# Filling the places behind the last edge on another engine, and issuing the products of types later, in a graph layer on one core

## The chip, the cores and the metric

The kernel runs on one core of a Trainium2 chip. The metric is the device time of one execution in microseconds (us). The kernel before takes 2105.05 us, the median of 3 runs (2102.25 to 2107.07).

A core has engines that run their own instruction streams in order and wait for one another by semaphores: TensorE (PE in the profile, its weight loads as PEld), VectorE (DVE), ScalarE (ACT), GpSimd (POOL) and SyncE (SP), which here issues plain transfers. Indirect transfers, that is gathers by a list of row numbers, are issued by GpSimd.

## The reference

There are 12500 nodes with 256 features each and 212500 edges, sorted by their target `dst`; each edge has a source and one of 8 types.

```python
h = jnp.maximum(_layernorm(x, axis=-1), 0.0)
hx = jnp.einsum('ni,rio->rno', h, weight)          # 8 x 12500 x 256
msg = hx[edge_type, src]
agg = segment_sum(msg, dst, num_segments=12500)
out = x + agg * 0.5**0.5 + h_bias + (h @ loop_weight) * 0.5**0.5
```

The last 12500 edges before the sort were loops from each node to itself; the sort is stable, so the loop of a node is the last of its edges. A loop has a type like any other edge.

## The kernel before

**Tiles of edges.** The kernel first writes h to memory (`norm_rows`), and then takes the edges in 1603 tiles of at most 128. Two tiles make a unit. For tile t, GpSimd gathers the 128 source rows of h (`gather`, L683), VectorE builds a one-hot of target and type for four tiles at once (`onehots`, L696), TensorE multiplies rows by one-hot into a PSUM bank of the unit (`edge_sums`, L723: two products, which the profile shows as four records), and VectorE adds the bank to a ring `acc` of sums by node and type in on-chip memory (`add_sums`, L735). There are four such banks.

The gather of tile t+58 (`AHEAD`) is written in the program in front of the work of tile t. There are buffers for 62 tiles (`MSGS`). The one-hots are made 8 tiles or more ahead (`LEAD`).

**Groups of nodes.** When all the edges of 128 nodes are in the ring, the group's output is made: 18 products with the weights and the loop weight (`product`, L883), handed out by a queue with due tiles among the tiles that follow. `finish` runs three tiles (`REST`) after the last of them. It adds the products to x (L894, L895), issues the store, and opens the slot of group g+6 in the ring: `begin` turns the rows of h of that group on TensorE into the bank `pt` (L759), copies them to `self_t` on ScalarE (L762), and in eight instructions on VectorE (L773) writes the loop's message, by its type, as the first summand. So loops are not gathered. There are 98 groups.

**Types of the loops.** `begin` has to know the type of each node's loop. For four groups at a time, `mark` prepares 0/1 patterns on VectorE; `find_types` multiplies them by a list of kinds (L800, into bank `pt`), finds the kind of each node in six small VectorE operations (L805 to L815), and writes four diagonal matrices on ScalarE (L818); `spread_types` turns these by one product (L825) and a copy (L827) into a row of types for all lanes. The bank `pt` has one buffer, which the turned rows, the products of types and the transposes of the preparation share. `find_types` is called in `finish` of every fourth group, after `begin`; `spread_types` is put into a list `late` with a due tile three tiles on. Entries of `late` are run in order once their tile is reached.

**Rounds of preparation.** Lists of rows, columns and places are made in 7 rounds of 128 units. Round b is prepared from 184 tiles (`PREP`) in front of its first tile: `load_indices` loads pieces of `src`, `dst` and `edge_type_8` into `nat_s`, `nat_d`, `nat_t`; `rises` (L366) subtracts neighbouring targets, and further VectorE steps follow, three steps every two tiles. The first three steps (the loads, `rises`, `stays`) stand in the same tile. In the last round not all of the 128 rows have edges: 33 rows are full, one has 41 edges and the others none. There the three arrays are filled first, and then loaded over. The fill of `nat_d` has to rise along the row, so that there are no edges with equal targets in it.

The work order on each engine is the order in which the program issues it.

Of the kernel before, what the change touches and what calls it, by code (L numbers as in the profile page):

```python
# [13 lines left out]
ALU = mybir.AluOpType  # L14
# [14 lines left out]
EDGES = 267  # L29
# [23 lines left out]
REST = 3  # L53
# [156 lines left out]
def kernel(  # L210
# [11 lines left out]
    nc = tc.nc  # L222
    N, D = x.shape
# [10 lines left out]
    EU = plan.EU  # L234
# [21 lines left out]
    line = const.tile([P, XG * GROUP], F32, name="line")  # L256
# [13 lines left out]
    with ExitStack() as main:  # L270
# [33 lines left out]
        def load_indices(b):  # L304

            rows_ = min(P, NU - b * P)
            last = b == NB - 1
            full = rows_ - last
            size = EDGES if b else U
            e0 = P * U + (b - 1) * P * EDGES if b else 0  # L310
            nat = {}
            for name, a, more in (("s", src, 0), ("d", dst, 1 if b else 0), ("t", etype, 0)):
                n = ep.tile([P, EDGES + 1], I32, name=f"nat_{name}")
                if last:

                    if more:
                        nc.gpsimd.iota(
                            n, pattern=[[2, EDGES + 1]], base=N - 2 * EU, channel_multiplier=0)
                    else:
                        nc.vector.memset(n, -1 if name == "d" else 0)  # L320
                if full:
                    nc.sync.dma_start(n[:full, : size + more], bass.AP(
                        tensor=a.tensor, offset=a.offset + e0, ap=[[size, full], [1, size + more]]))
                if last:
                    nc.sync.dma_start(
                        n[full : full + 1, :EU], a[E - EU : E].rearrange("(p q) -> p q", p=1))
                nat[name] = n
            return nat
# [416 lines left out]
        def clear(g):  # L745

            s0 = g % SLOTS * GROUP
            a = acc[:, :, :, s0 : s0 + GROUP].rearrange("p c r d -> p (c r) d")
            i = nc.scalar.activation(a, zero.unsqueeze(2).to_broadcast([P, KC * R, GROUP]), AF.Copy)
            zeroed[g, "slot"] = i.ins  # L750
# [14 lines left out]
        def begin(g):  # L765

            n = plan.ends[g] - plan.starts[g]
            q, k = divmod(g, XG)
            pst, copy = turn_nodes(g, selves)
            of = typed[q][:, k * GROUP : k * GROUP + n].unsqueeze(1).to_broadcast([P, KC, n])  # L770
            s0 = g % SLOTS * GROUP
            for r in range(R):
                i = nc.vector.scalar_tensor_tensor(  # L773
                    acc[:, :, r, s0 : s0 + n], of, float(r + 1), pst[:, :, :n],
                    op0=ALU.is_equal, op1=ALU.mult)
                if r == 0:
                    tc.add_manual_dep(i.ins, copy.name, SYNC_DEP, reason="one reader at a time")
            zeroed[g, "slot"] = i.ins
# [14 lines left out]
        def find_types(q):  # L793

            pt = ps_d.tile([P, 512], F32, tag="pt", name="ptt")
            pt = pt[:, : XG * (LASTS + 2)].rearrange("p (g k) -> p g k", g=XG)
            parts = [(b, m, i) for b, m in marked.pop(q) for i in range(2)]
            for g in range(XG):
                for b, m, i in parts:
                    nc.tensor.matmul(  # L800
                        pt[:, g, :], m[:, i, g * GROUP : (g + 1) * GROUP], loops[b][:, i, :],
                        start=(b, m, i) == parts[0], stop=(b, m, i) == parts[-1])

            place_ = small.tile([P, XG], F32, name="place_")
            nc.vector.tensor_scalar(  # L805
                place_, pt[:, :, LASTS], float(-plan.starts[XG * q]), None, op0=ALU.add)
            nc.vector.tensor_tensor(place_, place_, pt[:, :, LASTS + 1], op=ALU.add)
            nc.vector.tensor_tensor(place_, node, place_, op=ALU.subtract)
            one = small.tile([P, XG, LASTS], F32, name="one")
            nc.vector.tensor_tensor(  # L810
                one, line[:, :LASTS].unsqueeze(1).to_broadcast([P, XG, LASTS]),
                place_.unsqueeze(2).to_broadcast([P, XG, LASTS]), op=ALU.is_equal)
            nc.vector.tensor_tensor(one, one, pt[:, :, :LASTS], op=ALU.mult)
            kinds = small.tile([P, XG], F32, name="kinds")
            nc.vector.tensor_reduce(kinds, one, AX.X, ALU.add)  # L815
            marked[q] = marks.tile([P, XG * GROUP], BF16, name="diagonal")
            for g in range(XG):
                nc.scalar.activation(  # L818
                    marked[q][:, g * GROUP : (g + 1) * GROUP], ident, AF.Copy,
                    scale=kinds[:, g : g + 1])  # L820

        def spread_types(q):

            pt = ps_d.tile([P, 512], F32, tag="pt", name="ptt")
            nc.tensor.matmul(pt, ones_b, marked.pop(q), start=True, stop=True)  # L825
            typed[q] = types.tile([P, XG * GROUP], BF16, name="types")
            nc.scalar.activation(typed[q], pt, AF.Copy)  # L827
# [42 lines left out]
        def group_work(g):  # L870

            d0, n = plan.starts[g], plan.ends[g] - plan.starts[g]
            s0 = g % SLOTS * GROUP
            first_dep = [True]

            def product(r, c):
                if (r, c) == (R, 0):
                    got["out", g] = outs[g % 2][:, 0, :]
                if r == R:
                    lhs, rhs = got["self", g][:, c, :n], wl[:, c, :]  # L880
                else:
                    lhs, rhs = acc[:, c, r, s0 : s0 + n], w[:, c, r * D : (r + 1) * D]
                i = nc.tensor.matmul(got["out", g][:n], lhs, rhs, start=(r == R and c == 0),  # L883
                                     stop=(r == R - 1 and c == KC - 1))
                if (r, c) == (R, 0) and g < 2:
                    tc.add_manual_dep(i.ins, done["bias"], SYNC_DEP, reason="one engine at a time")
                if r < R and first_dep[0]:
                    first_dep[0] = False
                    tc.add_manual_dep(i.ins, added[plan.last[g]].name, SYNC_DEP, reason="sums complete")

            def finish():
                q, k = divmod(g, XG)
                rows_ = got["x", q]
                nc.vector.tensor_add(rows_[:n, k, :], rows_[:n, k, :], outs[g % 2][:n, 1, :])  # L894
                nc.vector.tensor_add(rows_[:n, k, :], rows_[:n, k, :], got["out", g][:n])  # L895
                if XG * (q + 1) >= plan.NG:
                    nc.sync.dma_start(out[d0 : d0 + n], rows_[:n, k, :])
                elif k == XG - 1:
                    first = plan.starts[XG * q]
                    nc.sync.dma_start(  # L900
                        out[first : d0 + n].rearrange("(k p) d -> p k d", p=P), rows_)
                b = g + SLOTS
                q, k = divmod(b, XG)
                if b < plan.NG:
                    if q < plan.typed:
                        clear(b)
                    else:
                        begin(b)
                if q + 1 >= plan.typed and XG * (q + 1) < plan.NG:
                    if k == XG // 4:  # L910
                        load_groups("h", h32, q + 1)
                    if k == XG - 2:
                        mark(q + 1)
                    if k == XG - 1:
                        find_types(q + 1)
                        done["late"].append((done["tile"] + REST, lambda: spread_types(q + 1)))

            def last():
                done["late"].append((done["tile"] + REST, finish))

            work = []
            for r in [R, *range(R)]:
                for c in range(KC):
                    work.append((0.55, lambda r=r, c=c: product(r, c)))
            work.append((0.0, last))
            return work

        with tc.manual_schedule():
# [46 lines left out]
            done = {"norm": 0, "weights": False, "late": [], "tile": 0}  # L975
# [39 lines left out]
            late = done["late"]  # L1015
# [113 lines left out]
```

## Time and profile before

| | |
|---|---|
| median of 3 runs | 2105.05 us |
| profiled execution, its own time | 2107.2 us |
| its span | 2105.2 us |
| TensorE busy | 1789.1 us, 85% |
| VectorE busy | 1327.7 us, 63% |
| GpSimd busy | 1523.2 us, 72% |
| ScalarE busy | 218.5 us, 10% |
| TensorE clock granted, mean | 0.92 of full speed |
| chain that ended last | TensorE 67%, VectorE 13%, issue 6%, transfers 6%, GpSimd 4% |

Times in the profile are counted from the start of the span. The slices are 40 equal parts of the span, 52.6 us each, with the busy share of an engine in tenths. A row of the waits has the waiting instruction, what released it, the total in us, the number of times and the longest. A row of the timeline has the start, the duration, the engine, the line, what is written and read, and in brackets the idle time of the engine before it and what ended it; a "q" behind an engine is its sequencer, where transfers are issued. A row of a table by stage has the stage, its length, for each engine the busy time and in brackets the number of records, then the granted TensorE clock, the transfers' share and their GB/s.

### The profile page before, as it was taken

The numbers are of one execution on the slowest core, as the hardware profiler recorded it, in microseconds if no ns is written. First come the engines' busy times: TensorE is split into PE (matmuls) and PEld (weight loads), VectorE is DVE, ScalarE is ACT, GpSimd is POOL, SyncE is SP. The second block draws the span as 40 slices with busy tenths as digits, with TensorE's granted clock in tenths as the row PEclk, the third lists the DMA queues.
The fourth block names the chain that finished last, engine by engine and source line by source line (L and its number), as shares of the span: only waits on it lengthen the run. The fifth ranks groups of instructions, "written<-read, shape, count | busy, mean of one in ns | idle before, by whom it ended". The sixth has DMA issues, their size and how long they took to land.

```text
span 2105.2 us, 29382 instructions
## 1 busy us (share of the span) xinstructions
PE 1789.1 (85%) x10411; PEld 1644.1 (78%) x10411; DVE 1327.7 (63%) x3274; ACT 218.5 (10%) x470; POOL 1523.2 (72%) x1630
## 2 busy tenths in 40 slices
PE   2468999998999998999988998988998860799998
PEld 2357998888898888888877887877888750698897
DVE  7869666668666687665686655577665520856652
ACT  7854100000000000000000000000000000000000
POOL 7767777777777777777777777777777777677750
PEclk8578999998999999999999999999999985899999
DMA  8963443443444344344344344343443433343430
GB/s 297 373 208 103 145 136 106 136 144 106 135 136 135 105 142 135 106 135 136 106 143 131 109 135 135 107 143 106 135 135 106 135 106 106 117 127 105 130 91 15
DMA packets 146904, 281.17 MB, mean 134 GB/s; under 512 B 28125, under 2 KB 95460, under 8 KB 146756
## 3 DMA queue, kind: packets, MB, share of 16 engines
q0 software_dynamic: 76944, 210.21, 34.2%
q1 hardware_dynamic: 69812, 69.05, 10.2%
q8 instruction: 85, 1.39, 0.3%
q14 instruction: 63, 0.52, 0.1%
HBM read 253.55 MB, written 25.60 MB: 133 GB/s over the span
## 4 chain that ended last, share of the span: by engine, by line
PE 67%; DVE 13%; issue 6%; DMA 6%; POOL 4%; ACT 2%; SPq 0%; DVEq 0%; ACTq 0%; POOLq 0%
PE ps L723 34%; PE po L883 31%; DMA msg<-h,gidx 4%; POOL msg L683 4%; DVE acc L773 3%; DVE acc L735 2%; DVE moves L349 2%; DVE fixed L350 2%; DMA h<-xt 1%; ACT xt L645 1%; DVE oh L696 1%; PE pst L759 1%; DMA w<-in_L_gnn_weight_dram 1%; DVE n_stats L633 0%; PE ptt L800 0%
## 5 line engine op out<-in xcount | busy, mean ns | idle before, releaser
L683 POOL DMA_INDIRECT msg<-h,gidx x1507 | 1430.0, 949 | 481.7 <-issue 396.3
L723 PE MATMUL ps<-oh,msg 128*128 128x176 f32 (+1 forms) x6412 | 1146.2, 310 | 187.5 <-DVE acc L735 76.6
L723 PEld LDWEIGHTS ps<-oh,msg 128*128 128x128 f32 x6412 | 1056.2, 198 | 290.1 <-issue 100.9
L883 PE MATMUL po<-w,acc 128*128 128x256 f32 x3136 | 892.7, 387 | 0.0
L696 DVE TENSOR_TENSOR oh<-fixed,cols 128x704 f32<-128x704 f32 x402 | 356.0, 886 | 356.2 <-PE ps L723 349.3
L883 PEld LDWEIGHTS po<-w,acc 128*128 128x128 f32 x3136 | 547.4, 195 | 25.3
L735 DVE TENSOR_TENSOR acc<-acc,ps 128x352 f32 x802 | 412.9, 515 | 180.9 <-PE ps L723 171.9
L773 DVE SCALAR_TENSOR_TENSOR acc<-types,pst 128x256 f32<-128x256 bf16 (+1 forms) x688 | 234.8, 414 | 74.5 <-ACT self_t L762 73.0
L762 ACT ACTIVATE self_t<-pst 128x256 f32<-128x256 f32 x98 | 37.5, 383 | 1524.5 <-PE pst L759 1524.5
L883 PE MATMUL po<-wl,self_t 128*128 128x256 f32 x392 | 121.2, 438 | 3.9 <-ACT self_t L762 2.4
L683 POOL DMA_INDIRECT msg<-in_x_dram,gidx x96 | 90.9, 947 | 31.1 <-issue 26.2
L883 PEld LDWEIGHTS po<-wl,self_t 128*128 128x128 f32 x392 | 75.7, 214 | 11.9 <-ACT self_t L762 2.8
L800 PE MATMUL ptt<-loops,mark 128*128 128x24 bf16 x216 | 9.3, 179 | 80.8 <-DVE acc L773 80.8
L800 PEld LDWEIGHTS <-mark 128*128 128x128 bf16 x216 | 7.3, 101 | 85.7 <-DVE acc L773 85.7
L366 DVE TENSOR_TENSOR rise<-nat_d 128x267 f32<-128x267 int32 x6 | 2.6, 432 | 79.0 <-DMA nat_d<-in_dst_dram 79.0
L645 ACT ACTIVATE xt<-xt,n_shift,n_rstd 128x256 f32<-128x256 f32 x98 | 50.9, 589 | 11.0 <-DVE n_shift L642 11.0
L645 ACT ACTIVATE msg<-msg,e_shift,e_rstd 128x256 f32<-128x256 f32 x96 | 49.6, 589 | 8.5 <-DVE e_shift L642 8.1
L894 DVE TENSOR_TENSOR xr<-xr,po 128x256 f32<-128x256 f32 x98 | 40.4, 412 | 7.4 <-PE po L883 7.4
L895 DVE TENSOR_TENSOR xr<-xr,po 128x256 f32<-128x256 f32 x98 | 41.2, 421 | 3.4
L818 ACT ACTIVATE diagonal<-ident,kinds 128x128 bf16<-128x128 f32 x88 | 28.1, 390 | 113.8 <-DVE kinds L815 113.8
L759 PE MATMUL pst<-ident,hr 128*128 128x128 f32 x196 | 37.7, 274 | 0.4 <-DVE offs L586 0.2
L349 DVE TENSOR_SCALAR moves<-fixed 128x267 int32<-128x267 int32 x84 | 36.4, 433 | 1.7
(200 smaller groups left out, 402.3 us busy)
## 6 DMA issues: line engine op xcount, KB each, us to landing
msg<-h,gidx POOLq DMA_INDIRECT x1507, 2.8
xt<-in_x_dram SPq DMA_DIRECT2D x24, 512.0 KB, 6.4
h<-xt SPq DMA_DIRECT2D x24, 512.0 KB
xr<-in_x_dram SPq DMA_DIRECT2D x24, 512.0 KB, 7.1
hr<-h SPq DMA_DIRECT2D x24, 512.0 KB, 6.3
out_dram<-xr SPq DMA_DIRECT2D x24, 512.0 KB, 4.0
w<-in_L_gnn_weight_dram SPq DMA_DIRECT2D x2, 1024.0 KB, 8.3
msg<-in_x_dram,gidx POOLq DMA_INDIRECT x96, 5.8
```

The lines of the kernel that those rows point to most:

```text
L349: nc.vector.tensor_single_scalar(m, packed, 1 << (bit + k), op=ALU.bitwise_and)
L350: nc.vector.copy_predicated(packed[:, : EDGES - (1 << k)], m[:, 1 << k :], packed[:, 1 << k :])
L645: nc.scalar.activation(rows_[j], rows_[j], AF.Relu, bias=shift[:n, j : j + 1], scale=rstd[:n, j : j + 1])
L683: nc.gpsimd.indirect_dma_start(out=msg[t], out_offset=None, in_=table[:, :], in_offset=bass.IndirectOffsetOnAxis(ap=gidx[b][:, at : at + 1 ...
L696: nc.vector.tensor_tensor(o[:, k : k + v, :i, :], iota_f.unsqueeze(1).unsqueeze(1).to_broadcast([P, v, i, C]), of.unsqueeze(3).to_broadcas ...
L723: nc.tensor.matmul(ps[:, c, from_ : from_ + width], m[:, c * P : (c + 1) * P], o[:, :width], start=(i == 0 and c == 0), stop=(end and c == ...
L735: i = nc.vector.tensor_tensor(a, a, ps, op=ALU.add)
L759: nc.tensor.transpose(pst[:, c, :n], rows_[:n, c * P : (c + 1) * P], ident[:n, :n])
L773: i = nc.vector.scalar_tensor_tensor(acc[:, :, r, s0 : s0 + n], of, float(r + 1), pst[:, :, :n], op0=ALU.is_equal, op1=ALU.mult)
L883: i = nc.tensor.matmul(got["out", g][:n], lhs, rhs, start=(r == R and c == 0), stop=(r == R - 1 and c == KC - 1))
L894: nc.vector.tensor_add(rows_[:n, k, :], rows_[:n, k, :], outs[g % 2][:n, 1, :])
L895: nc.vector.tensor_add(rows_[:n, k, :], rows_[:n, k, :], got["out", g][:n])
```

## The change

The fill of `nat_d` in the last round is made by a `tensor_scalar` on VectorE instead of an iota on GpSimd; both write N - 2 EU + 2k at place k of each row. `line` holds 0, 1, 2, ... as floats. `find_types`, which was called at once in `finish`, is put into `late` with a due tile three tiles on; `spread_types`, which was due three tiles on, is due six tiles on.

```diff
@@ load_indices
                 if last:
                     if more:
-                        nc.gpsimd.iota(
-                            n, pattern=[[2, EDGES + 1]], base=N - 2 * EU, channel_multiplier=0)
+                        nc.vector.tensor_scalar(
+                            n, line[:, : EDGES + 1], 2.0, float(N - 2 * EU), op0=ALU.mult, op1=ALU.add)
                     else:
                         nc.vector.memset(n, -1 if name == "d" else 0)
@@ group_work, finish
                     if k == XG - 2:
                         mark(q + 1)
                     if k == XG - 1:
-                        find_types(q + 1)
-                        done["late"].append((done["tile"] + REST, lambda: spread_types(q + 1)))
+                        done["late"].append((done["tile"] + REST, lambda: find_types(q + 1)))
+                        done["late"].append((done["tile"] + 2 * REST, lambda: spread_types(q + 1)))
```

In the issued order the streams of ScalarE and SP are unchanged. GpSimd's loses the iota, which stood behind the gather of tile 1410; the 192 gathers behind it move up by that one instruction. VectorE's gains one instruction at tile 1352, between two memsets. On TensorE and VectorE the operations of `find_types`, and on TensorE L825, stand three tiles later in each of 22 places.

## Prediction

> **What bounds the kernel now.** I read the page's slices first, then the waits, then the timeline around the longest wait, then tables of single lines by stage, and last the end of the timeline.
>
> ```profile
> span 2105.2 us, 29382 instructions
> ...
> PE   2468999998999998999988998988998860799998
> ...
> DVE  7869666668666687665686655577665520856652
> POOL 7767777777777777777777777777777777677750
> ```
>
> The PE line here is the one point to look at: full nearly everywhere, but it falls to 6 and 0 in slices 34 and 35, where VectorE falls to 2 and 0, while GpSimd goes on at 7. GpSimd is at 0 in the last slice, TensorE is not: the gathers end before the products.
>
> ```profile
> DVE rise L366 <- DMA nat_d<-in_dst_dram: 79.0, 2, 74.4
> PE ptt L800 <- DVE acc L773: 80.8, 21, 7.8
> PE ps L723 <- DVE acc L735: 76.6, 11, 66.6
> PE ps L723 <- DMA msg<-h,gidx: 27.1, 41, 2.0
> POOL msg L683 <- PE ps L723: 51.8, 129, 5.0
> ```
>
> Columns: total us, times, longest. Both parts of the change aim at a row here. One wait of 74.4 us at L366 drags TensorE into one of 66.6 us. The 21 waits of L800 are 3.8 us each. The row of 41 waits for gathers says that TensorE at times catches up with GpSimd.
>
> ```profile
> 1710.22 0.28 DVE L320 MEMSET nat_t<- 128x268 int32 x1
> ...
> 1781.65 0.95 POOL L683 DMA_INDIRECT msg<-h,gidx  x1 [0.30 <-issue]
> 1782.61 0.37 POOL L317 IOTA nat_d<- 128x268 int32 x1
> 1783.00 0.29 SPq L322 DMA_DIRECT2D nat_d<-in_dst_dram  x1
> ...
> 1784.86 0.44 DVE L366 TENSOR_TENSOR rise<-nat_d 128x267 f32<-128x267 int32 x1 [74.36 <-DMA nat_d<-in_dst_dram]
> ```
>
> The wait is a matter of order. The iota stands on GpSimd behind the gathers of the next 58 tiles, and TensorE was at that moment only a few tiles behind the gathers. So VectorE sits from 1710.5 until GpSimd has issued 58 gathers (58 x 1.25 = 72.7 us), then the load of `nat_d` takes 1.9 us more.
>
> ```profile
> 213.00:1710.00 1497.00, 1133.03 (x1194) 0.96 0.43 127
> ...
> 1860.00:2036.00 176.00, 133.04 (x142) 0.97 0.43 126
> ```
>
> That is L683 alone on GpSimd: 1497/1194 = 1.2538 us a gather, about 0.95 busy and 0.30 of issue, with no wait over 0.3 us between 260 and 1780. GpSimd runs at a pace of its own.
>
> ```profile
> 1860.00:2036.00 176.00, 107.33 (x624) 100.24 (x623) 0.97 0.43 126
> 2036.00:2105.00 69.00, 29.68 (x174) 27.39 (x172) 0.99 0.05 16
> ```
>
> That is L723 alone on TensorE, four records a tile: 156 tiles in 176 us, 1.128 us a tile with its products, faster than a gather by 0.126 us. Yet 174/4 = 43 tiles are still unmultiplied when the last gather goes out. These are the backlog from the wait: the end is set by TensorE working it off.
>
> ```profile
> 1709.19 0.95 POOL L683 DMA_INDIRECT msg<-h,gidx  x1 [0.30 <-issue]
> 1712.12 0.83 PE L723 MATMUL ps<-oh,msg 128*128 128x176 f32 x4 [0.20 <-DMA msg<-h,gidx]
> ...
> 2035.77 0.95 POOL L683 DMA_INDIRECT msg<-h,gidx  x1 [0.31 <-issue]
> 2077.78 0.65 PE L723 MATMUL ps<-oh,msg 128*128 128x144 f32 x4
> ...
> 2100.66 0.42 DVE L895 TENSOR_TENSOR xr<-xr,po 84x256 f32<-84x256 f32 x1
> ```
>
> The first two are gather and matmuls of the same tile (1352, counted from 0): 2.9 us apart, the least in this trace, so TensorE was as close behind as it can be. The third is the last gather (tile 1602). The fourth is tile 1597; from there to the span's end are 2105.2 - 2077.8 = 27.4 us of TensorE work, mostly the last products, and the last rows.
>
> **The change, part by part.**
>
> *The fill.* Removed: one iota of 0.37 us on GpSimd, and with it the order "58 gathers, iota, load, VectorE". Added: one `tensor_scalar` over 128x268 on VectorE, between the memsets of `nat_s` and `nat_t`. The nearest rows are tensor_scalar of L524 (128x256, 0.38 us) and L349 (128x267, 0.43); I take 0.40. The loads of `nat_d` and `nat_t` on SP now wait for VectorE alone. SP is free for them: it issued both loads of `nat_s` by 1710.86. So the loads of `nat_d` go out at about 1710.9 and L366 starts 1.9 us later, as from 1783.00 to 1784.86. That is a new wait of some 2 us on VectorE. Its bounds are 0 (the loads of earlier rounds stood on SP without a fill, and four of five such L366 never waited) and 4.64 us (the other one, near 1392, with 512 KB transfers ahead of it on SP). Behind it on VectorE are one-hots made two quads ahead and sums whose PSUM banks are four deep, so a wait of this size eats into TensorE's slack and not into the end.
>
> A rule speaks against handing this to VectorE. Rows first: over 1507 gathers the shortest, median and longest are 0.940, 0.946 and 1.272 us, beside 3274 VectorE instructions, so a collision has cost at most 0.33 us; I take 0 and keep 0.33. The Trainium skill, "SBUF — State Buffer", section "Who interferes with whom", says that a tensor_scalar can run in a mode that locks GpSimd out of a shared port, and its section "A bandwidth-pool intuition that's wrong" has a GpSimd-issued transfer go from about 620 to 3100 ns by it. By that the end would be some 2.5 us later, once; the rows here show no such case.
>
> *What GpSimd does then.* After 1709.19 there are 250 gathers to issue. At 1.2538 us the last starts at 2022.6; reading the flag at L602 (0.51 us on GpSimd) makes it 2023.1. Today it starts at 2035.77. The 12.7 us between are waits for buffers that TensorE released late after the long wait (15.6 us in 12 rows for L723 between 1700 and 1870); with no backlog they have no cause, and the flag comes before GpSimd asks for it.
>
> *What TensorE does then.* What is late next is the gather: TensorE goes back to waiting for each one, as before 1710. Does its own work allow that? From tile 1352 to the end it needs, without the wait, about 70 us for 48 tiles (the same stretch one round earlier, 1375 to 1444, with that round's preparation), 233.4 us for tiles 1400 to 1602 (1856.5 to 2089.9) and 15.3 us after: 1712.1 + 318.7 = 2030.8. The gathers bound it later than that, so it catches up. Near the end tiles carry four product records each and take 1.4 us (2068 to 2077), so it drops about 1.2 us behind. The sum: tile 1597's gather starts at 2023.1 - 5 x 1.254 = 2016.8; matmuls 2.9 + 1.2 us later at 2020.9; 27.4 us of tail give a span of 2048.3, against 2105.2: **-56.9 us**.
>
> *The products of types.* Nothing is added; eight matmuls of L800, six small VectorE operations, four copies of L818 stand three tiles later, and L825/L827 too. No DMA moves. On TensorE, L800 waits today until VectorE has done the eight L773 that read the PSUM bank it writes (2.74 us plus 0.7 before them). Three tiles are 3.4 to 3.75 us, so that wait should fall from 3.3 us to 0 to 1 us. On VectorE, L805 and five more now come after three tiles' one-hot and sums; they wait for L800, which TensorE reaches after the same tiles, and VectorE is idle 37% of the time. What it is worth: in front of 1710 the gathers cover it, since TensorE had caught up several times between 770 and 1710 with these waits in place; it catches up sooner and then waits for data. After 1710 three places remain (about 3.3 us each, 10 us) and gathers cover those as well. I take **0**; the bounds are -10 us, which only counts if TensorE sets the end, and +4 us, if a place close to the end lost the three tiles it gained.
>
> *Sum.* -56.9 + 0. Against the profiled execution's own time, 2107.2 us (span 2105.2 and 2.0 around it), 2050.3. It lies 2.15 us above the median of the runs (2105.05), so on the scale of the median 2048.
>
> **The rivals.**
>
> *TensorE stays behind.* The last round's preparation (some 40 VectorE operations and their transposes) costs lag; the earlier one took it from 7 to 12 us within 40 tiles. If that and the waits for groups are not worked off, the end is later by up to 12 us: 2053 to 2062. Against it: 0.126 us a tile over 250 tiles is 31 us. Waits of TensorE for `msg` would then be missing after 1760.
>
> *The wait returns at another place.* VectorE waits for a load behind large transfers, or the flag or an index column arrives late. For it: 6.52 us for such a load near 1390. A wait of 15 to 45 us in place of 74, beyond what the slack takes, gives 2065 to 2095. Against it: no other GpSimd instruction stands between VectorE and this round.
>
> *Slower: the types come too late.* The next group's transposes stand 13 tiles behind L825 today and will stand 10 behind (2 instead of 5 in the first two places). L773 needs the types, and everything on VectorE queues behind it. If the chain took over ten tiles (12.5 us), each of 22 places would wait up to the three tiles lost, 22 x 3.75 = 82 us, all in front of gathers if they hid none: 2130. Against it: the copy L827 starts at most 4.6 us after ACT becomes free and takes 0.6; the first two places lie where GpSimd is far ahead (160 gathers and 396/4 = 99 tiles by 213 us), and the gathers' pace would hide most of it.
>
> *No change.* If the wait were only the gathers' own limit, removing it would move nothing. For it: GpSimd works on throughout. Against it: 43 tiles of backlog at the last gather.
>
> **How the numbers follow.** The likeliest case, gathers set the pace to the end, 0.80: 2043 to 2053 (2.5 us that the runs differ by, and the fill's new wait). TensorE behind 0.11. Another wait 0.03. Slower 0.03. No change 0.02. Something better than the gathers' pace 0.01. The range takes in the first two: 2042 to 2060. 0.2% of this kernel, 4 us, is about what a measurement can tell. Faster 0.95, same 0.02, slower 0.03.
>
> **What would show it.** Right: no wait of L366 over 7 us; the iota's row gone and a VectorE row of about 0.4 us in its place; the last gather at about 2023; waits for GpSimd's data on TensorE in the slices after 34, and under 10 tiles of L723 left when the last gather starts; L800's wait under 1 us a place, with the freed time showing up as waits for `msg`. Wrong: if the last gather comes much earlier or later than 2023, if L366 still waits tens of us, or if TensorE has tens of tiles left at the end, which would make its own pace the bound and the types' 10 us count.

## The result and the profile after

The changed kernel takes 2049.23 us, the median of 6 runs (2047.77 to 2052.66), against 2105.78 us (6 runs, 2102.25 to 2107.08) for the kernel before, measured on the same chip. The ratio is 0.9734, with a 95% interval of 0.9721 to 0.9747: 2.7% faster. The forecast was 2048 us. The profiled execution has a span of 2046.1 us and took 2047.77 us.

The slices of the page:

```profile
span 2046.1 us, 29386 instructions
...
PE   2468999997999989989887989897998898999998
...
DVE  7869666668666668655558655558665557755642
POOL 7767777777777777777777777777777777777773
```

The hole, which lies in slices 33 and 34, is gone on TensorE and VectorE. TensorE has as many slices of 9 (23) and of 8 (11) as before, and three of 7: the slices do not tell whether it has time to spare, the waits do. GpSimd has work up to the last slice.

The waits (total us, times, longest):

```profile
DVE rise L366 <- DMA nat_d<-in_dst_dram: 5.5, 2, 3.2
PE ptt L800 <- DVE acc L773: 6.2, 2, 3.5
PE ps L723 <- DVE acc L735: 16.3, 22, 2.8
PE ps L723 <- DMA msg<-h,gidx: 81.3, 132, 4.2
```

The wait of 74.4 us has become one of 3.2. The 21 waits of L800 (80.8 us) have become two (6.2 us). TensorE's waits for gathers have risen from 27.1 us in 41 places to 81.3 in 132: time that TensorE won is spent waiting for data.

The timeline around the fill:

```profile
1707.41 0.23 DVE L317 TENSOR_SCALAR nat_d<-line 128x268 int32<-128x268 f32 x1
...
1708.49 0.29 SPq L322 DMA_DIRECT2D nat_d<-in_dst_dram  x1
...
1711.10 0.44 DVE L366 TENSOR_TENSOR rise<-nat_d 128x267 f32<-128x267 int32 x1 [3.17 <-DMA nat_d<-in_dst_dram]
```

The fill takes 0.23 us, and the load goes out 0.8 us after it ends. Of the 3.17 us of wait that are left, 2.6 are the load itself.

L723 by stage, as in the prediction (four records a tile), and the end of the timeline:

```profile
1860.00:2020.00 160.00, 92.34 (x510) 78.08 (x510) 1.00 0.41 118
2020.00:2046.00 26.00, 3.24 (x19) 2.75 (x17) 0.95 0.13 41
```

```profile
1706.84 0.95 POOL L683 DMA_INDIRECT msg<-h,gidx  x1 [0.30 <-PE ps L723]
...
2018.74 0.65 PE L723 MATMUL ps<-oh,msg 128*128 128x144 f32 x4
...
2020.23 1.09 POOL L683 DMA_INDIRECT msg<-h,gidx  x1 [0.30 <-issue]
...
2041.61 0.42 DVE L895 TENSOR_TENSOR xr<-xr,po 84x256 f32<-84x256 f32 x1
```

When the last gather starts, 19 records are left, five tiles, where it was 43 tiles. The first row is the gather of tile 1352, the third the last one: 313.4 us for 250 gathers, 1.2536 us each. The second is tile 1597, and from there to the end it is 27.4 us, as before.

### The profile page after: what moved, and what is told of

Its sections match the earlier page's. It is cut to its first block, busy times and chain, and to the rows that moved or that the text cites. A ratio compares the mean times of both kernels' runs of the same rounds, so it can differ in the third digit from the quotient of the medians.

```text
span 2046.1 us, 29386 instructions
## 1 busy us (share of the span) xinstructions
PE 1795.5 (88%) x10411; PEld 1602.1 (78%) x10411; DVE 1324.3 (65%) x3275; ACT 218.4 (11%) x470; POOL 1522.6 (74%) x1629
## 4 chain that ended last, share of the span: by engine, by line
PE 50%; DMA 15%; DVE 12%; issue 11%; POOL 8%; ACT 3%; DVEq 0%; SPq 0%; ACTq 0%; POOLq 0%
PE ps L723 27%; PE po L883 22%; DMA msg<-h,gidx 12%; POOL msg L683 8%; DVE acc L735 2%; DVE acc L773 2%; DVE moves L349 1%; DMA h<-xt 1%; DVE fixed L350 1%; ACT xt L645 1%; DVE oh L696 1%; PE pst L759 1%; DMA w<-in_L_gnn_weight_dram 1%; ACT msg L645 0%; DVE n_stats L633 0%
## 5 line engine op out<-in xcount | busy, mean ns | idle before, releaser
L723 PE MATMUL ps<-oh,msg 128*128 128x176 f32 (+1 forms) x6412 | 1159.2, 310 | 185.3 <-DMA msg<-h,gidx 81.3
L723 PEld LDWEIGHTS ps<-oh,msg 128*128 128x128 f32 x6412 | 1029.9, 195 | 340.3 <-issue 68.5
L883 PEld LDWEIGHTS po<-w,acc 128*128 128x128 f32 x3136 | 539.3, 193 | 27.8 <-issue 4.0
L773 DVE SCALAR_TENSOR_TENSOR acc<-types,pst 128x256 f32<-128x256 bf16 (+1 forms) x688 | 234.9, 414 | 111.5 <-ACT self_t L762 110.5
L883 PE MATMUL po<-wl,self_t 128*128 128x256 f32 x392 | 102.6, 384 | 3.9 <-ACT self_t L762 2.4
L883 PEld LDWEIGHTS po<-wl,self_t 128*128 128x128 f32 x392 | 67.8, 193 | 9.8 <-ACT self_t L762 2.8
L350 DVE COPY_PREDICATED fixed<-moves,fixed 128x266 int32<-128x266 int32 (+6 forms) x84 | 33.7, 401 | 2.9
L633 DVE BATCH_NORM_STATS2 n_stats<-xt 128x6 f32<-128x256 f32 x98 | 34.4, 411 | 1.1 <-issue 0.7
L633 DVE BATCH_NORM_STATS2 e_stats<-msg 128x6 f32<-128x256 f32 x96 | 33.5, 412 | 0.0
```

The source lines that it names most:

```text
L350: nc.vector.copy_predicated(packed[:, : EDGES - (1 << k)], m[:, 1 << k :], packed[:, 1 << k :])
L633: nc.vector.bn_stats(stats[:n, j, :], rows_[j])
L723: nc.tensor.matmul(ps[:, c, from_ : from_ + width], m[:, c * P : (c + 1) * P], o[:, :width], start=(i == 0 and c == 0), stop=(end and c == ...
L773: i = nc.vector.scalar_tensor_tensor(acc[:, :, r, s0 : s0 + n], of, float(r + 1), pst[:, :, :n], op0=ALU.is_equal, op1=ALU.mult)
```

## The experiments

My theory was: the long wait comes from the place of the iota in GpSimd's stream; what it left behind was a backlog that TensorE could not work off before the end; without it the gathers' pace sets the end, and then the types' places are worth nothing. The rivals were that the fill's engine matters, that the types carry a part of the gain, and that TensorE's own work sets the end.

**The fill alone.** The kernel before with the first hunk only.

```diff
-                        nc.gpsimd.iota(
-                            n, pattern=[[2, EDGES + 1]], base=N - 2 * EU, channel_multiplier=0)
+                        nc.vector.tensor_scalar(
+                            n, line[:, : EDGES + 1], 2.0, float(N - 2 * EU), op0=ALU.mult, op1=ALU.add)
```

> Only the fill goes to VectorE; find_types and spread_types stay where the kernel before has them. Theory (the fill removes the long wait, after which the gathers' pace sets the end and covers the places of the types): 2048 to 2052 us, as the changed kernel. Rival (the types' places still count, 3 of them behind tile 1352 at 3.3 us each, or all 22): 2056 to 2060, or more.

Measured: 2053.34 us, beside 2109.12 for the kernel before on that chip; ratio 0.9734 (0.9718 to 0.9751), that of the whole change. Its waits:

```profile
PE ptt L800 <- DVE acc L773: 82.6, 21, 8.7
PE ps L723 <- DMA msg<-h,gidx: 33.5, 49, 2.9
```

All 21 waits at L800 are still there and cost nothing: TensorE has 33.5 us of waits for gathers in place of 81.3. Beside the fill, the types are worth 0 within the intervals of the two ratios, some 4 us.

**The types alone.** The kernel before with the second hunk only.

```diff
-                        find_types(q + 1)
-                        done["late"].append((done["tile"] + REST, lambda: spread_types(q + 1)))
+                        done["late"].append((done["tile"] + REST, lambda: find_types(q + 1)))
+                        done["late"].append((done["tile"] + 2 * REST, lambda: spread_types(q + 1)))
```

> Only find_types and spread_types go three and six tiles later; the iota stays on GpSimd. The long wait of L366 stays at about 74 us. Theory (TensorE sets the end behind that wait, so the three places behind it count there with 3.3 us each): 2093 to 2098 us. Rival (they are worth nothing wherever they stand): 2105. A second rival (all 21 waits of 3.8 us count): 2025.

Measured: 2094.4 us against 2109.12, ratio 0.9931 (0.9914 to 0.9947), 11 to 18 us faster. The long wait stays:

```profile
DVE rise L366 <- DMA nat_d<-in_dst_dram: 77.7, 2, 75.0
```

So the same edit is worth nothing where gathers set the pace and some 15 us where TensorE does. In the profiled execution, the fastest of its four, L366 starts 1.7 us earlier than in the kernel before (1783.14 for 1784.86) and the span is 18.9 us shorter, so 17.2 us are won behind L366, where three of the 21 places stand. It is more than the three waits of 3.3 us that I had allowed; the fifth experiment is on that.

**The iota earlier on GpSimd.** The kernel before, with the iota still on GpSimd but written 30, or 64, tiles earlier in the program. The loads stay where they were.

```diff
+        def fill_last():
+            n = ep.tile([P, EDGES + 1], I32, name="nat_d")
+            nc.gpsimd.iota(n, pattern=[[2, EDGES + 1]], base=N - 2 * EU, channel_multiplier=0)
+            filled.append(n)
...
             def blocks_ahead(t):
+                if t == U * (NB - 1) - PREP - 30:
+                    fill_last()
```

> The kernel before with the same iota on GpSimd, but written 30 tiles earlier in the program (a place 28 gathers ahead of TensorE's tile instead of 58). Theory (the wait is the number of gathers in front of the iota): L366 waits 74.4 - 30 x 1.25 = 37 us, and the end comes some 37 us earlier: 2065 to 2072 us. Rival (what costs is that GpSimd makes the fill, or its collision with VectorE): 2105, the wait unchanged.

> The same iota on GpSimd, written 64 tiles earlier, so that its gathers in front are done before VectorE asks. Theory: no wait over 5 us at L366 and the time of the fill on VectorE alone, 2048 to 2052 us. Rival (the engine of the fill matters): 2060 or more.

Measured with 30: 2070.96 us against 2109.12, ratio 0.9822 (0.9805 to 0.9838). With 64: 2053.64 us, ratio 0.9733 (0.9716 to 0.9749). The timeline and the waits of the first (the added lines move L366 to L370 and L317 to L308):

```profile
1746.17 0.37 POOL L308 IOTA nat_d<- 128x268 int32 x1
...
DVE rise L370 <- DMA nat_d<-in_dst_dram: 41.1, 2, 36.7
```

and of the second:

```profile
1705.79 0.37 POOL L308 IOTA nat_d<- 128x268 int32 x1
...
1716.84 0.44 DVE L370 TENSOR_TENSOR rise<-nat_d 128x267 f32<-128x267 int32 x1 [3.33 <-DMA nat_d<-in_dst_dram]
```

The wait falls by 30 x 1.25 us, as the number of gathers in front does, and with 64 the iota is done before VectorE asks. The time is then that of the fill on VectorE. So the engine of the fill does not matter, its place does. On the chip of these runs, the first 37.6 us of wait that go (74.4 to 36.7) give back 38 us (2109.12 to 2070.96); the next 33 us give 17 (2053.64). There the gathers take over as the bound: after 1715, TensorE waits 1.2 us for them with 30 places and 12.5 us with 64.

**The types one tile later.** The kernel before with `find_types` one tile later, so that L800 waits a little less.

```diff
-                        find_types(q + 1)
-                        done["late"].append((done["tile"] + REST, lambda: spread_types(q + 1)))
+                        done["late"].append((done["tile"] + 1, lambda: find_types(q + 1)))
+                        done["late"].append((done["tile"] + 1 + REST, lambda: spread_types(q + 1)))
```

> The kernel before with find_types one tile later and spread_types four (iota on GpSimd, so TensorE sets the end behind the long wait). In the kernel before each of the three places behind it waits 3.31 us at L800 and then has a granted clock of 0.50 for some 4 us (1839 to 1843), where TensorE needs 2 us for what takes 1. Theory (the clock's fall comes from the length of the wait and is a second cost of some 2.4 us a place): with a wait of about 2.1 us the clock stays at 1.0 and three places cost 6 us in place of 17; 2094 to 2098 against 2105 (ratio 0.994 to 0.997). Rival (the clock falls after any wait): 3 x 1.2 us, 2101 to 2102, ratio 0.998. Rival (only the waits cost, the clock nothing): the same 2101 to 2102, but with the clock at 1.0 behind L800.

Measured: 2097.93 us against 2106.93, ratio 0.9967 (0.9949 to 0.9986), 3 to 11 us faster. In the traces the granted clock changes only at steps of a grid of 3.41 us. TensorE by these steps around the first of the three places, in the kernel before (length, busy, records, granted clock, transfers' share, GB/s), and the wait in it:

```profile
1834.37:1837.79 3.42, 1.38 (x11) 1.00 0.31 97
1837.79:1841.20 3.41, 2.13 (x13) 0.50 0.40 115
1841.20:1844.61 3.41, 3.41 (x12) 0.50 0.14 38
1844.61:1848.03 3.42, 3.42 (x22) 1.00 0.12 38
...
1839.07 0.39 PE L800 MATMUL ptt<-loops,mark 128*128 128x24 bf16 x8 [3.31 <-DVE acc L773]
1839.30 2.05 PE L883 MATMUL po<-wl,self_t 128*128 128x256 f32 x4
```

and in this kernel, the same place and the two later ones:

```profile
1836.64:1840.06 3.42, 1.57 (x16) 1.00 0.40 116
1840.06:1843.47 3.41, 3.41 (x11) 0.50 0.28 78
1908.32:1911.74 3.42, 1.57 (x14) 1.00 0.37 98
1911.74:1915.15 3.41, 3.41 (x34) 1.00 0.31 96
1976.59:1980.00 3.41, 2.62 (x17) 1.00 0.39 115
1980.00:1983.42 3.42, 2.37 (x20) 1.00 0.38 115
...
1839.56 0.36 PE L800 MATMUL ptt<-loops,mark 128*128 128x24 bf16 x8 [1.85 <-DVE acc L773]
1839.77 1.79 PE L883 MATMUL po<-w,acc 128*128 128x256 f32 x4
...
1911.59 0.57 PE L800 MATMUL ptt<-loops,mark 128*128 128x24 bf16 x16 [1.85 <-DVE acc L773]
1981.05 0.36 PE L800 MATMUL ptt<-loops,mark 128*128 128x24 bf16 x8 [1.85 <-DVE acc L773]
```

In the kernel before each of the three waits of 3.31 us brings one or two steps at half clock: four product records that take 1.03 us at full clock take 2.05, 2.05 and 1.63. With 1.85 us of wait this happens in one place of three. Two tiles' edge sums and products take 2.82 us at full clock (1833.89 to 1836.71 in the kernel with the types alone), and behind the three waits 5.51, 5.69 and 4.58 in the kernel before, so the lowered clock adds 2.7, 2.9 and 1.8 us. A place costs some 5.7 us, not 3.3; three cost 17.3 (9.9 of waits and 7.4 of clock). In this kernel they cost 3 x 1.85 + 1.8 = 7.4. The difference of 10 us lies within the 3 to 11 measured, and 17.3 within the 11 to 18 of the types alone. From the start of L366 to the end of the span it is 320.4 us in the kernel before, 310.8 in this one and 303.2 with the types alone: 9.6 and 17.2 us less. Neither of my theories fits entirely: the lowered clock is a second cost, but a wait of 1.85 us can bring it too. The last section says more on what decides it.

**More work on TensorE.** The changed kernel, with the first loop product of each group from the third on issued two, or eight, more times ahead of the one that counts.

```diff
+                if (r, c) == (R, 0) and g > 1:
+                    for _ in range(2):
+                        nc.tensor.matmul(got["out", g][:n], lhs, rhs, start=True, stop=True)
                 i = nc.tensor.matmul(got["out", g][:n], lhs, rhs, start=(r == R and c == 0),
```

> The changed kernel, with the first loop product of each group (from group 2) issued two more times before it counts: 2 x 0.43 us of TensorE work for each of 96 groups, 82 us in all, 0.05 us a tile. Theory (the gathers set the pace and leave TensorE 0.126 us a tile): hidden but for the last two groups, 1 to 4 us longer than the changed kernel, ratio to before 0.974 to 0.976. Rival (TensorE's own work sets the end): 82 us longer, ratio 1.01.

> The same with eight more: 3.4 us a group, 329 us in all, 0.21 us a tile, more than the slack of 0.126. Theory: TensorE becomes the bound from start to end and GpSimd waits for buffers; 1443 tiles from 274 us at 1.32 to 1.34 us and 34 us of tail, 2200 to 2245 us. Rival (TensorE has much more slack than 0.126 us a tile): under 2100.

Measured with two: 2051.95 us against 2106.93, ratio 0.974 (0.9724 to 0.9756). 82 us of added work on TensorE do not show; its waits for gathers fall to 43.3 us. With eight: 2181.58 us, ratio 1.0357 (1.0337 to 1.0378). L723 in the kernel with eight, from 300 to 1700:

```profile
300.00:1700.00 1400.00, 740.99 (x4356) 692.45 (x4356) 1.00 0.42 123
```

That is 1089 tiles in 1400 us, 1.286 us a tile: TensorE is the bound and GpSimd waits. It came out 18 us under the range I gave. Less the added 0.21 us, TensorE's own pace is 1.076 us a tile, so that in the changed kernel it has 0.178 us a tile to spare, not 0.126.

**More work on GpSimd.** The changed kernel, with four small iotas behind every 16th gather.

```diff
                     gather(t + AHEAD)
+                    if t % 16 == 0 and t >= 224:
+                        for _ in range(4):
+                            nc.gpsimd.iota(extra, pattern=[[2, 64]], base=0, channel_multiplier=0)
```

> The changed kernel, with four small iotas on GpSimd into a tile of their own behind every 16th gather, from tile 282 on, 83 times. Each four should lengthen the gap between two gathers by some 0.6 us (between the rows of 0.138 us for 7 and 0.37 us for 268 elements, with part of the issue gap of 0.30 beside them), 40 to 70 us in all. Theory (the gathers' pace sets the end): the last gather and the span move by the same amount, 2090 to 2120 us. Rival (TensorE sets the end): the span moves by less than a third of the last gather's shift.

Measured: 2118.11 us against 2106.93, ratio 1.0056 (1.0034 to 1.0078). The iotas in the list of groups, and the last gather:

```profile
L1037 POOL IOTA extra<- 128x64 int32 x332 | 62.2, 187 | 17.5
...
2088.96 0.94 POOL L684 DMA_INDIRECT msg<-h,gidx  x1 [0.30 <-PE ps L724]
```

The last gather starts 68.7 us later than in the changed kernel (2088.96 for 2020.23) and the span is 67.8 us longer (2113.9 for 2046.1). What GpSimd loses, the kernel loses, one for one; 82 us on TensorE cost it about nothing.

## Why the prediction was right

*The wait and its cause.* Shown. Moved by 30 places it falls by 37.6 us; moved by 64, or made on VectorE, it is down to some 3 us. The part that I forecast for VectorE's new wait, 2 us with bounds of 0 and 4.64, is 3.17. The load of `nat_d` did not go out at 1.9 but at 2.6 us before L366. The fill took 0.23 us, not 0.40; neither reaches the end.

*The gathers after it.* 313.4 us for 250 gathers were forecast and measured. That the last one starts at 2020.2 and not at 2023.1 is due to where the count began: tile 1352's gather stands at 1706.84 in this execution and at 1709.19 in that of before, and reading the flag did not add its 0.5 us.

*TensorE catches up.* It does: it multiplies tile 1597 4.8 us after its gather, where 4.1 was forecast, and the tail is 27.4 us in both. The span of 2046.1 is 2.2 us under the sum of 2048.3; it is the fastest of the six runs, and their median lies 1.2 us over the forecast. But its slack was mis-sized: I took TensorE's own pace of 1.128 us from a stretch with two of the L800 places in it, which with their clock cost 5.7 us each and not 3.3. The added work shows 1.076. The error was on the safe side. Two readings were off without weight: the hole lies in slices 33 and 34, and 2.9 us from a gather to its matmuls is not the least of that trace, which is 2.7.

*The types.* 0 beside the fill: shown by the fill alone, with the same ratio to four digits. The bound of -10 us "if TensorE sets the end" was too small by the term of the clock: the types alone gave 11 to 18 us there. The wait at L800 fell as forecast, but for two places in which it is still up to 3.5 us.

*The rivals.* TensorE does not stay behind: it is 11.3 us behind the gather at tile 1380 and 2.8 at tile 1444. No other wait has taken the place; the longest that are new on TensorE, 6.4 us at L336 (1112.8) and 5.4 at L825 (487.4), stand once each, in front of tile 1352. The types do not come late: VectorE's waits ahead of L773 end on the copy `self_t`, as before (110.5 us in 58 places for 73.0 in 49), and the time with the types moved is that without.

*The rule on the shared port.* In this execution the gathers take 0.942 us at the least, 0.946 at the median and 1.246 at the most. The gather that runs during the fill (1706.84) takes 0.95, and so does the next (1708.10). The Trainium skill, "SBUF — State Buffer", section "A bandwidth-pool intuition that's wrong", has a GpSimd-issued transfer of about 620 ns take about 3100 beside a VectorE copy. The gathers' durations here show no such case.

## What to carry to other kernels

An instruction that is written where its result is needed is not done there if its engine runs through a queue of prefetches in order: here a 0.37 us fill cost 56 us because 58 gathers stood in front of it. Look, for the engine that prefetches, at what else is in its stream and who waits for that; moving the instruction to another engine, or far enough up in the same stream, is worth the same (64 places here; 30 gave 38 of the 56 us). Before adding up the waits that an edit removes, ask which engine sets the pace at that place: the same edit was worth 0 where the gathers set the pace to the end, and some 15 us, nearly all from three of its 21 waits, where TensorE did.

## What the runs showed that was not expected

A short wait of TensorE can cost more than its length. With each of three waits of 3.31 us the granted clock fell to half for one or two steps of 3.41 us, which added 1.8 to 2.9 us; with three of 1.85 us it fell once, for one step, and added 1.8.

The traces show most of what decides it: the clock of a step follows how busy TensorE was in the step before. Counted from 260 us on in all ten traces, a step at full clock with TensorE busy for less than 0.41 of it was followed by half clock in all of 170 cases, one with 0.53 or more in none of 4730, and one between in 27 of 85. A step at half clock was followed by full clock in all of 191 cases with 0.85 or more busy, in none of 137 with less than 0.79, and in 6 of 13 between. So it counts how a wait lies on the grid. At the third place of the kernel with the types one tile later, the wait of 1.85 us spans two steps and leaves TensorE busy for 2.62 and 2.37 us of them. At the first and the second it falls into one and leaves 1.57 us, 0.46 of the step: there the clock fell once and stayed once, and what decides between the two the runs do not show.

"TensorE: Matmul & The Clock Gate", section "What's actually happening", in the Trainium skill, has the array go to half clock after an idle window of about 3.4 us, and says that the window runs freely. The half clock and the length of the window agree with the 0.50 and the 3.41 us here. That the window has to be idle does not agree: one that was busy for 1.38 of 3.42 us was enough.
